# Attention with scores and weighted sums in turns, in three stretches of key tiles

## The chip, the cores and the metric

The kernel runs on one core of a Trainium2 chip. The core has a matrix engine (TensorE, PE in the profile, with its weight loads as PEld), a vector engine (VectorE, DVE), an engine for activations (ScalarE, ACT), a general one (GpSimd, POOL) and one that issues most DMAs (SyncE, SP). Each engine runs its own queue of instructions in order and waits on semaphores for the others. Matmuls write to PSUM, eight banks of 512 float32 values per partition; everything else lies in SBUF. The metric is the device time of one execution in microseconds, the median of several runs.

## What is computed

One transformer block on 2048 rows of 256 values: cross-attention with 16 heads of 64 over 1601 context rows plus one learned null key and value, with a residual, then a feed-forward part with weights of +1 and -1.

```python
x = layernorm(x);  a = layer_norm(x, g_norm)
q = a @ Wq;  k, v = split(context @ Wkv)            # 16 heads of 64
k = concat(null_k, k);  v = concat(null_v, v)       # 1602 keys
sim = (q * s) @ (k * s).T                           # s = 64 ** -0.25, masked
out = softmax(sim) @ v
x = x0 + layer_norm(out @ Wout, g_out)
h = relu(s0 * concat(y, -y) @ w(k0)) * 2            # y = layernorm(x), w = +-1
x = x + s2 * (relu(s1 * h @ w(k1)) * 2) @ w(k2)
```

## The kernel before

The attention part works in 32 units. A unit is a pair of heads p (eight of them) and a block b of 512 query rows (four of them). Keys come in 13 tiles of 128 (the last has 66), counted by k.

For a unit, `exps` (L284) computes the transposed scores of key tile k: two heads side by side in the rows of the array, 64 each, into a PSUM tile sT of two banks, and ACT takes the exponential into an SBUF tile e. The first two tiles also add a shift (L307) so that the exponential stays in range, and the stored keys are differences, so the shift stays in the accumulating banks for later tiles. `weighted` (L312) multiplies e with the values and adds over all 13 tiles in one PSUM tile av; two heads lie side by side in the columns of the array. GpSimd adds the 13 tiles e into acc (L498, L500), the denominators before the last sum over partitions.

The shift of a unit is the maximum of its scores, found one unit earlier: `max_chunk` (L251) computes the scores of 128 queries and some 400 keys in the faster float32r, and DVE reduces them; 16 chunks make a unit. `max_combined` (L264) joins them, `max_turned` (L269) turns them to rows and multiplies with `fan`, a stored 128 x 4 x 128 pattern of ones and zeros, into mT.

PSUM has two pools of two tiles each, two banks to a tile: `spare` (sT, av, po) and `flex` (max chunks, den, mt, psq). A tile is taken in turn, and its first writer waits until the last reader of the tile before it is done.

All of this stands in a schedule written by hand: the order in the program is the order on every engine. The loop over units (from L463) does, for each unit:

- 13 times `exps`, each with one max chunk of the next unit behind it, two behind tiles 0, 4 and 8 (`extra`)
- `max_combined` for the next unit, and in units 0 and 1 the normalisation of input rows two blocks ahead (`input_normed`), in unit 30 that of a finished block
- 13 times `weighted`; after tile 2, `divided` (L331) of the unit before: den on PE (L334), then on DVE the reciprocal (L336) and the product with avs (L337) into aoT
- in units 28 and 29 the weights w0 of the feed-forward part (L526, L528), in unit 0 some small scalars
- ACT copies av into avs (L542); then the projections of the next pair's values and keys (in blocks 0, 1 and 2), `project_out` of the unit before (po, L324, added into y_sb at L329), `max_turned`, and `project_q` for the unit after the next (psq at L196, then ACT writes qr at L197 and qT at L198)

qr is what the max chunks of the next unit but one read; qT is what its scores read. The feed-forward part follows after the last unit, with its own order (from L627).

Of the kernel before, what the change touches and what calls it, by code (L numbers as in the profile page):

```python
# [22 lines left out]
HEADS, DH = 16, 64  # L23
# [12 lines left out]
def xattn_ffn(ctx, tc, x, ctxT, mask, g_norm, null_kv, wq, wkv, wout, g_out, k0, k1, k2, s0, s1, s2, out):  # L36
# [12 lines left out]
    def spare(name):  # L49
        return ps_s.tile([128, 2, 512], F32, tag="s", name=name)  # L50
# [52 lines left out]
    def norm_root(b):  # L103
        mv, r = norms[b]
        nc.scalar.activation(r, mv[:, :, 1], AF.Sqrt, bias=eps_sb)
# [37 lines left out]
    with ExitStack() as att:  # L143
# [12 lines left out]
        maskb = ap.tile([128, KC], F32, name="maskb")  # L156
        ones_r = ap.tile([128, 128], F32R, name="ones_r")
        mcol = ap.tile([128, 128], F32, name="mcol")
        fan = ap.tile([128, 4, 128], F32, name="fan")
        pick = ap.tile([128, 4], F32, name="pick")  # L160

        weights = {}

# [105 lines left out]
        def max_turned(p, b):  # L269

            ps = flex(f"mt_{p}_{b}")
            nc.tensor.transpose(ps[:, 0, :128], mcol, ident)
            shifts[p, b] = wp.tile([128, 512], F32R, tag="mT", name=f"mT_{p}_{b}", bufs=1)
            nc.vector.tensor_tensor(
                shifts[p, b].rearrange("p (t q) -> p t q", t=4),
                ps[:, 0:1, :128].to_broadcast([128, 4, 128]),
                fan,
                ALU.mult,
            )

        def rows_of(k):
            return 128 if k < KC - 1 else KLAST
# [26 lines left out]
            nc.scalar.activation(e[:n], ps[:n], AF.Exp, bias=maskb[:n, k : k + 1])  # L309
            return e  # L310

        def weighted(p, k, e, av):  # L312
            v = pairs[p][1]
            n = rows_of(k)
            for j in range(2):
                nc.tensor.matmul(  # L316
                    av[ts(j, DH), 0, :], v[:n, k, ts(j, DH)], e[:n, j, :], start=k == 0, stop=k == KC - 1
                )

        def project_out(p, b, aoT):  # L320
            po = spare(f"po_{p}_{b}")
# [6 lines left out]
            else:  # L328
                nc.vector.tensor_tensor(y, pv, y, ALU.add)  # L329

        def divided(p, b, avs, acc, ps):  # L331

            for j in range(2):
                nc.tensor.matmul(ps[ts(j, DH), :], ones, acc[:, j, :], start=True, stop=True)  # L334
            aoT = lp.tile([128, 512], F32, tag="aoT", name=f"aoT_{p}_{b}", bufs=1)
            nc.vector.reciprocal(aoT, ps)  # L336
            nc.vector.tensor_tensor(aoT, avs, aoT, ALU.mult)  # L337
            return aoT

# [26 lines left out]
                nc.vector.tensor_scalar_mul(xnT[:, b, 1, :], pt[:, 1, :], gn_sb[:, 1:2])  # L366

        units = [(p, b) for p in range(NP) for b in range(NB)]
        extra = {0, 4, 8}

        ahead = {0: ((0, 1), (0,)), 1: ((2, 3), (1,)), 2: ((), (2, 3)), 3: ((), ())}

# [39 lines left out]
        nc.gpsimd.memset(mcol, 0.0)  # L412
        nc.gpsimd.memset(maskb, 0.0)
        nc.gpsimd.memset(ones, 1.0)
        nc.gpsimd.memset(fan, 1.0)

        nc.scalar.activation(warm, eps_sb, AF.Sqrt)

        open_pair(0)
        xn = input_root(0)  # L420
        nc.vector.tensor_scalar(ones_r, ident, 0.0, 1.0, ALU.mult, ALU.add)
        nc.vector.tensor_tensor(pick, ident[:, 0:4], ident[:, DH : DH + 4], ALU.add)
        input_normed(0, *xn)
        project_k(0, 0, slot)
        input_turned(0, slot)
# [17 lines left out]
        nc.vector.tensor_scalar(  # L443
            maskb[:KLAST, KC - 1 : KC], mcol_u8[:KLAST, KC - 1 : KC], -MASKED, MASKED, ALU.mult, ALU.add
        )
        for t in range(4):
            nc.vector.tensor_scalar_mul(fan[:, t, :], fan[:, t, :], pick[:, t : t + 1])
        for n in (2, 3):
            for t in range(4):
                max_chunk(0, 0, 4 * t + n, slot)  # L450
# [11 lines left out]
        with tc.manual_schedule():  # L462
            for u, (p, b) in enumerate(units):  # L463
                nxt = units[u + 1] if u + 1 < len(units) else None
                if b == 0 and p + 1 < NP:
                    load_pair(p + 1)
                    open_pair(p + 1)
                if u == len(units) - 5:
                    k0_u8 = xnT[:, 0].rearrange("p c q -> p (c q)").bitcast(U8)
                    k0_u8 = k0_u8.rearrange("p (c f) -> p c f", f=FF)  # L470
                    nc.sync.dma_start(out=k0_u8, in_=k0.rearrange("(c p) f -> p c f", p=128))
                if u == len(units) - 2:
                    k1_u8 = xnT[:, 2:4].rearrange("p b c q -> p (b c q)").bitcast(U8)
                    k1_u8 = k1_u8.rearrange("p (c f) -> p c f", f=FF)
                    k2_u8 = xnT[:, 1, 0, :].bitcast(U8).rearrange("p (c f) -> p c f", f=D)
                    nc.sync.dma_start(out=k1_u8, in_=k1.rearrange("(c p) f -> p c f", p=128))
                    nc.sync.dma_start(out=k2_u8, in_=k2.rearrange("(c p) f -> p c f", p=128))
                if nxt is None:

                    y0, x0 = y_sb[:, 0:4, :], x_sb[:, 0:4, :]  # L480
                    nc.gpsimd.tensor_tensor(y0, y0, gout_sb.unsqueeze(1).to_broadcast([128, 4, D]), ALU.mult)
                    nc.gpsimd.tensor_tensor(x0, x0, y0, ALU.add)

                es, n = [], 0
                acc = lp.tile([128, 2, 512], F32, tag="acc", name=f"acc_{p}_{b}")
                for k in range(KC):
                    if k == 0:

                        odd = spare(f"sT_{p}_{b}_1")
                        sT = [spare(f"sT_{p}_{b}_0"), odd]  # L490
                    es.append(exps(p, b, k, sT))
                    for _ in range(2 if k in extra else 1):
                        if nxt is not None:
                            max_chunk(*nxt, n)
                            n += 1
                    m = rows_of(k)
                    if k == 1:
                        nc.gpsimd.tensor_tensor(acc, es[0], es[1], ALU.add)  # L498
                    elif k > 1:
                        nc.gpsimd.tensor_tensor(acc[:m], acc[:m], es[k][:m], ALU.add)  # L500
                if nxt is not None:
                    max_combined(*nxt)
                else:
                    norm_begin(0, x_sb, "r")
                    norm_root(0)
                    norm_end(0, y_sb, x_sb, beside=True)
                if u == len(units) - 2:
                    norm_begin(0, y_sb, "y")
                    norm_root(0)
                    norm_end(0, y_sb, y_sb, beside=True)  # L510

                    nc.scalar.activation(warm, eps_sb, AF.Exp)
                if u < 2:
                    input_normed(u + 2, *input_root(u + 2), beside=True)
                    nc.scalar.activation(warm, eps_sb, AF.Exp)

                av = spare(f"av_{p}_{b}")
                for k in range(KC):
                    weighted(p, k, es[k], av)
                    if k == 2 and last is not None:  # L520
                        aoT = divided(*last, flex(f"den_{p}_{b}")[:, 0, :])
                if u in (len(units) - 4, len(units) - 3):

                    half = k0_u8[:, 2 * (len(units) - 3 - u) :, :][:, 0:2, :]
                    if u == len(units) - 4:
                        nc.vector.tensor_scalar_mul(w0, half, sgn[:, 0:1])  # L526
                    else:
                        nc.vector.scalar_tensor_tensor(  # L528
                            w0, half, sgn[:, 0:1], w0.bitcast(F32), ALU.mult, ALU.subtract
                        )  # L530
                        nc.vector.tensor_scalar_mul(s1b[:, 0:1], sgn[:, 1:2], 2.0)
                        nc.vector.tensor_scalar_mul(s1b[:, 1:2], sgn[:, 1:2], -1.0)
                if u == 0:


                    nc.vector.tensor_scalar(sgn, s_sb[:, 0:2], 0.0, None, ALU.is_ge)
                    nc.vector.tensor_scalar(sgn, sgn, 2.0, -1.0, ALU.mult, ALU.add)
                    nc.vector.tensor_tensor(s_sb[:, 0:2], s_sb[:, 0:2], sgn, ALU.mult)
                    nc.vector.tensor_scalar(s_out, s_sb[:, 0:1], s_sb[:, 1:2], 8.0, ALU.mult, ALU.mult)
                    nc.vector.tensor_tensor(s_out, s_out, s_sb[:, 2:3], ALU.mult)  # L540
                avs = lp.tile([128, 512], F32, tag="avs", name=f"avs_{p}_{b}", bufs=1)
                nc.scalar.copy(avs, av[:, 0, :])  # L542

                if u < 2:
                    input_turned(u + 2)
                if p + 1 < NP:
                    for n in ahead[b][0]:
                        project_v(p + 1, n, spare if n % 2 else flex)
                    for n in ahead[b][1]:
                        project_k(p + 1, n, spare if n % 2 else flex)  # L550
                    if b == 2:
                        keys_stepped(p + 1)
                if nxt is None:
                    uT = turned(0)
                if last is not None:
                    project_out(*last[:2], aoT)
                if nxt is not None:
                    max_turned(*nxt)
                if u + 2 < len(units):
                    project_q(*units[u + 2])  # L560
                last = (p, b, avs, acc)
# [134 lines left out]
```

## Time and profile before

| | us |
|---|---|
| median of 3 runs (1352.63 to 1354.06) | 1352.65 |
| the profiled execution | 1355.55 |
| its span | 1353.7 |

The profiled execution stands 0.2% above the median; the 1.9 us between its time and its span lie outside the instructions. Attention takes the span up to about 1163 us, the feed-forward part the rest. The costliest groups, with the columns line, engine and operation, tiles and shapes, count, then busy time in us and mean in ns, then idle time before them and what ended it:

```profile
L500 POOL TENSOR_TENSOR acc<-acc,e 128x1024 f32<-128x1024 f32 (+1 forms) x352 | 847.3, 2407 | 27.6
L262 DVE TENSOR_REDUCE mx<-max 128x2 f32<-128x800 f32 (+1 forms) x512 | 481.3, 988 | 70.9 <-PE max L259 61.2
L309 ACT ACTIVATE e<-sT,maskb 128x1024 f32<-128x1024 f32 (+1 forms) x416 | 460.0, 1115 | 64.0 <-PE sT L296 38.0
L296 PE MATMUL sT<-qT,kT 64*128 64x512 f32 (+1 forms) x1664 | 444.4, 612 | 1.6 <-ACT e L309 1.4
L316 PE MATMUL av<-e,v 128*64 128x512 f32 (+1 forms) x1664 | 369.5, 594 | 1.0
L259 PE MATMUL max<-kr,qr 64*128 64x400 f32 (+1 forms) x1024 | 285.7, 568 | 2.3 <-DVE mx L262 1.5
```

Matmuls overlap, so a mean of 612 ns is the length of one record, not what one costs in the stream; the chain of waits shows the cost. Idle time in a group is that of its engine just before the instructions.

### The profile page before, as it was taken

How to read it: one execution, taken by the hardware profiler on the slowest of the kernel's cores; microseconds unless marked ns; L12 is line 12 of the kernel's file. 1: busy time of each engine (PE TensorE's matmuls, PEld its weight loads, DVE VectorE, ACT ScalarE, POOL GpSimd, SP SyncE). 2: the span in 40 equal slices, each digit the busy share in tenths (PEclk: the TensorE clock that was granted, in tenths of full speed). 3: DMA queues.
4: the chain of work that ended last, by engine and by line, in shares of the span. 5: the costliest groups of instructions: out<-in, count | busy, mean ns of one | idle time of the engine just before them, and what ended most of it. 6: DMA issues, size and time to landing. Idle time of an engine off the chain costs nothing.

```text
span 1353.7 us, 16255 instructions
## 1 busy us (share of the span) xinstructions
PE 1329.3 (98%) x6528; PEld 664.6 (49%) x6528; DVE 880.7 (65%) x957; ACT 607.7 (45%) x655; POOL 994.8 (73%) x492
## 2 busy tenths in 40 slices
PE   6999999999999999999999999999999999999998
PEld 3544444444444444444444444444444443688887
DVE  5677776676667756686767656767676884464431
ACT  1666454445444454444544454454445557421220
POOL 4377987798888987798779877987798999711100
PEclk9799999999999999999999999999999999999999
DMA  5000000000000000000000000000000010000000
GB/s 136 4 1 7 0 1 8 8 1 0 8 1 7 1 1 8 7 1 1 7 8 1 1 8 8 0 1 5 0 16 1 1 39 0 1 0 16 16 16 16
DMA packets 14940, 12.31 MB, mean 9 GB/s; under 512 B 2240, under 2 KB 14784, under 8 KB 14864
## 3 DMA queue, kind: packets, MB, share of 16 engines
q1 hardware_dynamic: 13552, 9.70, 2.5%
q10 hardware_dynamic: 832, 1.23, 0.3%
q8 instruction: 51, 0.84, 0.3%
q0 software_dynamic: 480, 0.34, 0.1%
q14 instruction: 25, 0.20, 0.1%
HBM read 9.17 MB, written 2.10 MB: 8 GB/s over the span
## 4 chain that ended last, share of the span: by engine, by line
PE 93%; DVE 3%; ACT 2%; DMA 1%; issue 0%; POOL 0%; SPq 0%; ACTq 0%
PE sT L296 28%; PE av L316 27%; PE ps L592 10%; PE max L259 8%; PE psq L196 4%; PE po L324 4%; PE psv L230 3%; PE psk L207 3%; PE ps L615 2%; PE den L334 2%; ACT e L309 1%; PE sT L307 1%; DVE mx L262 1%; DMA x_sb<-in_x 1%; PE xT L361 0%
## 5 line engine op out<-in xcount | busy, mean ns | idle before, releaser
L500 POOL TENSOR_TENSOR acc<-acc,e 128x1024 f32<-128x1024 f32 (+1 forms) x352 | 847.3, 2407 | 27.6
L262 DVE TENSOR_REDUCE mx<-max 128x2 f32<-128x800 f32 (+1 forms) x512 | 481.3, 988 | 70.9 <-PE max L259 61.2
L309 ACT ACTIVATE e<-sT,maskb 128x1024 f32<-128x1024 f32 (+1 forms) x416 | 460.0, 1115 | 64.0 <-PE sT L296 38.0
L296 PE MATMUL sT<-qT,kT 64*128 64x512 f32 (+1 forms) x1664 | 444.4, 612 | 1.6 <-ACT e L309 1.4
L316 PE MATMUL av<-e,v 128*64 128x512 f32 (+1 forms) x1664 | 369.5, 594 | 1.0
L259 PE MATMUL max<-kr,qr 64*128 64x400 f32 (+1 forms) x1024 | 285.7, 568 | 2.3 <-DVE mx L262 1.5
L316 PEld LDWEIGHTS av<-e,v 128*64 128x64 f32 (+1 forms) x1664 | 116.7, 137 | 239.0 <-issue 219.3
L259 PEld LDWEIGHTS max<-kr,qr 64*128 64x128 f32 x1024 | 97.3, 186 | 187.2 <-DVE mx L262 149.7
L296 PEld LDWEIGHTS sT<-qT,kT 64*128 64x128 f32 (+1 forms) x1664 | 135.3, 181 | 104.8 <-ACT e L309 81.5
L498 POOL TENSOR_TENSOR acc<-e,e 128x1024 f32<-128x1024 f32 x32 | 75.5, 2358 | 147.6 <-ACT e L309 147.6
L542 ACT COPY avs<-av 128x512 f32<-128x512 f32 x32 | 18.8, 587 | 327.0 <-PE av L316 327.0
L336 DVE RECIPROCAL aoT<-den 128x512 f32<-128x512 f32 x31 | 104.1, 3357 | 70.0 <-PE den L334 70.0
L197 ACT ACTIVATE qr<-psq 128x512 fp32r<-128x512 f32 x32 | 19.1, 597 | 139.1 <-PE psq L196 139.1
L592 PE MATMUL ps<-h0hi,w 128*128 128x512 f32 x256 | 79.5, 392 | 0.0
L592 PE MATMUL ps<-h0lo,w 128*128 128x512 f32 x256 | 78.9, 389 | 0.0
L211 DVE TENSOR_TENSOR kT<-psk,keep 128x400 f32<-128x400 f32 (+1 forms) x32 | 18.4, 574 | 90.0 <-PE psk L207 89.8
L119 POOL TENSOR_TENSOR y_sb<-y_sb,gout_sb 128x256 f32<-128x256 f32 x12 | 9.3, 776 | 90.1 <-DVE y_sb L86 90.1
L581 DVE SCALAR_TENSOR_TENSOR h1lo<-ps,h1hi 128x1024 fp32r<-128x1024 f32 x16 | 19.6, 1224 | 69.0 <-ACT h1hi L580 69.0
L196 PE MATMUL psq<-xnT,wq 128*128 128x512 f32 x128 | 62.2, 610 | 0.6 <-DVE kT L211 0.6
L324 PE MATMUL po<-wo,aoT 128*128 128x256 f32 x256 | 61.5, 383 | 0.0
L329 DVE TENSOR_TENSOR y_sb<-po,y_sb 128x1024 f32<-128x1024 f32 x28 | 34.2, 1220 | 40.0 <-PE po L324 39.8
L580 ACT ACTIVATE h1hi<-ps 128x1024 fp32r<-128x1024 f32 x16 | 16.4, 1027 | 94.6 <-PE ps L592 94.6
(125 smaller groups left out, 1054.8 us busy)
## 6 DMA issues: line engine op xcount, KB each, us to landing
x_sb<-in_x SPq DMA_DIRECT2D x4, 512.0 KB, 8.7
out_x<-o SPq DMA_DIRECT2D x8, 256.0 KB, 2.1
wkv<-in_wkv SPq DMA_DIRECT2D x16, 96.0 KB, 2.1
wq<-in_wq SPq DMA_DIRECT2D x8, 128.0 KB, 2.3
wo<-in_wout SPq DMA_DIRECT2D x8, 128.0 KB, 2.1
xnT<-in_k SPq DMA_DIRECT2D x1, 1024.0 KB, 5.9
ctx_sb<-in_ctxT ACTq DMA_DIRECT2D x3, 300.0 KB, 7.9
xnT<-in_k SPq DMA_DIRECT2D x1, 512.0 KB, 3.9
```

Source lines behind the costliest of these rows:

```text
L196: nc.tensor.matmul(ps[:, 0, :], weights[p][0][:, c, :], xnT[:, b, c, :], start=c == 0, stop=c == 1)
L207: nc.tensor.matmul(ps[:, 0, :w], weights[p][1][:, c, 0, :], ctx_sb[:, c, keys], start=c == 0, stop=c == 1)
L259: nc.tensor.matmul(ps[:, j, :w], queries[p, b][1][rows, ts(t, 128)], pairs[p][2][rows, ds(start, w)], start=True, stop=True)
L262: nc.vector.tensor_reduce(maxima[p, b][:, t, :, c], ps[:, :, :w], AX.X, ALU.max)
L296: nc.tensor.matmul(ps[:n, j, :], kT[rows, ds(128 * k, n)], qT[rows, :], start=k < 2, stop=k >= 2, skip_group_check=k >= 2,)
L309: nc.scalar.activation(e[:n], ps[:n], AF.Exp, bias=maskb[:n, k : k + 1])
L316: nc.tensor.matmul(av[ts(j, DH), 0, :], v[:n, k, ts(j, DH)], e[:n, j, :], start=k == 0, stop=k == KC - 1)
L324: nc.tensor.matmul(pv[:, t, :], aoT[:, ts(t, 128)], weights[p][2], start=True, stop=True)
L336: nc.vector.reciprocal(aoT, ps)
L498: nc.gpsimd.tensor_tensor(acc, es[0], es[1], ALU.add)
L500: nc.gpsimd.tensor_tensor(acc[:m], acc[:m], es[k][:m], ALU.add)
L592: nc.tensor.matmul(ps[:, f, :], w(c)[:, ts(2 * g + f, 128)], parts[part][:, c, :], start=i == 0, stop=i == len(steps) - 1,)
```

## The change

The 13 key tiles are cut into three stretches. In each, some tiles of scores come first and then some of weighted sums: 4 and 3, 4 and 5, 5 and 5. The sums of a stretch have a PSUM tile of their own (flex, flex, spare): ACT copies the first into avs, DVE adds the other two to it. The max chunks are dealt out anew: one before tile 0 and one before tile 4 (`AHEAD`), the others behind tiles (`BEHIND`), none behind tiles 3 and 7. `divided` is parted: den and the reciprocal (`inverse`) come after the first weighted tile of the second stretch (k = 3), the product behind the scores of the third. The norms of units 0 and 1 stand behind the scores of the third stretch, that of unit 30 behind those of the second; `input_turned` comes after the projections. `fan` goes; mT is multiplied with `pick`, read again for each of the 128 columns. avs has two buffers.

```diff
-        fan = ap.tile([128, 4, 128], F32, name="fan")
-        pick = ap.tile([128, 4], F32, name="pick")
+        pick = ap.tile([128, 4, 1], F32, name="pick")
...
-                fan,
+                pick.to_broadcast([128, 4, 128]),
...
-        def weighted(p, k, e, av):
+        def weighted(p, k, e, av, start, stop):
...
+                nc.tensor.matmul(av[ts(j, DH), 0, :], v[:n, k, ts(j, DH)], e[:n, j, :], start=start, stop=stop)
...
-        def divided(p, b, avs, acc, ps):
+        def inverse(p, b, avs, acc, ps):
 
             for j in range(2):
                 nc.tensor.matmul(ps[ts(j, DH), :], ones, acc[:, j, :], start=True, stop=True)
             aoT = lp.tile([128, 512], F32, tag="aoT", name=f"aoT_{p}_{b}", bufs=1)
             nc.vector.reciprocal(aoT, ps)
+            return aoT
+
+        def divided(p, b, avs, acc, ps):
+
+            aoT = inverse(p, b, avs, acc, ps)
             nc.vector.tensor_tensor(aoT, avs, aoT, ALU.mult)
             return aoT
...
-        extra = {0, 4, 8}
+
+        STRETCHES = ((range(0, 4), range(0, 3)), (range(4, 8), range(3, 8)), (range(8, 13), range(8, 13)))
+
+        AHEAD = {0: 1, 4: 1}
+        BEHIND = {0: 1, 1: 2, 2: 1, 4: 1, 5: 2, 6: 1, 8: 1, 9: 1, 10: 1, 11: 1, 12: 2}
...
-        nc.gpsimd.memset(fan, 1.0)
...
-        for t in range(4):
-            nc.vector.tensor_scalar_mul(fan[:, t, :], fan[:, t, :], pick[:, t : t + 1])
...
-                for k in range(KC):
-                    if k == 0:
-
-                        odd = spare(f"sT_{p}_{b}_1")
-                        sT = [spare(f"sT_{p}_{b}_0"), odd]
-                    es.append(exps(p, b, k, sT))
-                    for _ in range(2 if k in extra else 1):
+                avs = lp.tile([128, 512], F32, tag="avs", name=f"avs_{p}_{b}")
+
+                odd = spare(f"sT_{p}_{b}_1")
+                sT = [spare(f"sT_{p}_{b}_0"), odd]
+
+                def chunks(count):
+                    nonlocal n
+                    for _ in range(count if nxt is not None else 0):
+                        max_chunk(*nxt, n)
+                        n += 1
+
+                for i, (scores, sums) in enumerate(STRETCHES):
+                    for k in scores:
+                        chunks(AHEAD.get(k, 0))
+                        es.append(exps(p, b, k, sT))
+                        chunks(BEHIND.get(k, 0))
+                        m = rows_of(k)
+                        if k == 1:
+                            nc.gpsimd.tensor_tensor(acc, es[0], es[1], ALU.add)
+                        elif k > 1:
+                            nc.gpsimd.tensor_tensor(acc[:m], acc[:m], es[k][:m], ALU.add)
+                    if i == 2:
                         if nxt is not None:
-                            max_chunk(*nxt, n)
-                            n += 1
...
+                            max_combined(*nxt)
+                        else:
+                            norm_begin(0, x_sb, "r")
+                            norm_root(0)
+                            norm_end(0, y_sb, x_sb, beside=True)
+                        if last is not None:
+                            nc.vector.tensor_tensor(aoT, last[2], aoT, ALU.mult)
+                        if u < 2:
+                            input_normed(u + 2, *input_root(u + 2), beside=True)
+                            nc.scalar.activation(warm, eps_sb, AF.Exp)
+                    if u == len(units) - 2 and i == 1:
+                        norm_begin(0, y_sb, "y")
+                        norm_root(0)
+                        norm_end(0, y_sb, y_sb, beside=True)
+
+                        nc.scalar.activation(warm, eps_sb, AF.Exp)
+                    av = (flex, flex, spare)[i](f"av_{p}_{b}_{i}")
+                    for k in sums:
+                        weighted(p, k, es[k], av, k == sums[0], k == sums[-1])
+                        if k == 3 and last is not None:
+                            aoT = inverse(*last, flex(f"den_{p}_{b}")[:, 0, :])
+                    if i == 0:
+                        nc.scalar.copy(avs, av[:, 0, :])
+                    else:
+                        nc.vector.tensor_tensor(avs, av[:, 0, :], avs, ALU.add)
...
-                avs = lp.tile([128, 512], F32, tag="avs", name=f"avs_{p}_{b}", bufs=1)
-                nc.scalar.copy(avs, av[:, 0, :])
-
-                if u < 2:
-                    input_turned(u + 2)
+
                 if p + 1 < NP:
...
+                if u < 2:
+                    input_turned(u + 2)
```

More of the change, by code (lines that the diff above doesn't have):

```diff
@@ L315, in weighted @@
             for j in range(2):
-                nc.tensor.matmul(
-                    av[ts(j, DH), 0, :], v[:n, k, ts(j, DH)], e[:n, j, :], start=k == 0, stop=k == KC - 1
-                )
+                nc.tensor.matmul(av[ts(j, DH), 0, :], v[:n, k, ts(j, DH)], e[:n, j, :], start=start, stop=stop)
         def project_out(p, b, aoT):
@@ L421, in xattn_ffn @@
         nc.vector.tensor_scalar(ones_r, ident, 0.0, 1.0, ALU.mult, ALU.add)
-        nc.vector.tensor_tensor(pick, ident[:, 0:4], ident[:, DH : DH + 4], ALU.add)
+        nc.vector.tensor_tensor(pick[:, :, 0], ident[:, 0:4], ident[:, DH : DH + 4], ALU.add)
         input_normed(0, *xn)
@@ L485, in xattn_ffn @@
                 acc = lp.tile([128, 2, 512], F32, tag="acc", name=f"acc_{p}_{b}")
-                for k in range(KC):
-                    if k == 0:
-                        odd = spare(f"sT_{p}_{b}_1")
-                        sT = [spare(f"sT_{p}_{b}_0"), odd]
-                    es.append(exps(p, b, k, sT))
-                    for _ in range(2 if k in extra else 1):
-                        if nxt is not None:
-                            max_chunk(*nxt, n)
-                            n += 1
[L496 to L512, printed above, removed]
-                if u < 2:
-                    input_normed(u + 2, *input_root(u + 2), beside=True)
-                    nc.scalar.activation(warm, eps_sb, AF.Exp)
@@ L517, in xattn_ffn @@
[L517 to L521, printed above, removed]
+                avs = lp.tile([128, 512], F32, tag="avs", name=f"avs_{p}_{b}")
[6 more added lines that the diff above has]
+                        n += 1
@@ L540, in xattn_ffn @@
                     nc.vector.tensor_tensor(s_out, s_out, s_sb[:, 2:3], ALU.mult)
-                avs = lp.tile([128, 512], F32, tag="avs", name=f"avs_{p}_{b}", bufs=1)
-                nc.scalar.copy(avs, av[:, 0, :])
-                if u < 2:
-                    input_turned(u + 2)
                 if p + 1 < NP:
```

## The prediction

> **What bounds the kernel now.** I read the page's shares and groups first, then the waits, then the chain of waits over one (pair, block) unit, because 98% of busy PE can hide stretched matmuls.
>
> ```profile
> PE 1329.3 (98%) x6528; PEld 664.6 (49%) x6528; DVE 880.7 (65%) x957; ACT 607.7 (45%) x655; POOL 994.8 (73%) x492
> ...
> PE 93%; DVE 3%; ACT 2%; DMA 1%; issue 0%; POOL 0%; SPq 0%; ACTq 0%
> ```
>
> ```profile
> PEld max L259 <- DVE mx L262: 149.7, 343, 1.4
> ...
> PEld sT L296 <- ACT e L309: 81.5, 197, 1.1
> ```
>
> So PE carries the chain, but in the score loop it is held by DVE (a max buffer comes free) and by ACT (a score buffer comes free). The chain of one unit gives the prices (start, length, what):
>
> ```profile
> 609.94 1.29 PE av L316 x6
> 611.23 1.92 PE po L324 x8
> 613.15 0.11 PE mt L272
> 613.26 1.72 PE psq L196 x4
> 614.98 1.06 PE sT L296 x4
> 616.04 0.23 PE sT L307
> ...
> 618.86 0.18 PE max L259
> 619.04 1.12 PE sT L296 x4
> 620.16 0.18 PE max L259 x2
> 620.34 0.93 PE sT L296 x4
> 621.27 0.61 PE max L259 x4
> 621.88 0.86 PE sT L296 x4
> ...
> 630.24 1.12 ACT e L309
> 631.37 0.04 issue
> 631.41 2.79 PE av L316 x11
> ```
>
> Prices on PE: a key tile of scores 0.86 us, of weighted sums 4 x 0.215 = 0.86, the shift 0.23, a max chunk 0.18. What exceeds them is waiting: 1.12 and 0.93 for scores are ACT, 0.61 for two chunks instead of 0.36 is DVE. A third excess has no waiter: the first score tile after psq takes 1.06 where 0.86 is its price, and po takes 1.92 for eight matmuls of 0.215 (1.72). Each time the tiling of the array changes (128 rows x 128 columns to 64 rows, 64 columns to 128), 0.20 us go.
>
> From one psq end to the next a unit without projections of the next pair takes 32.4 us (the one from 1037.69 to 1070.11): scores 16.38, sums with the denominator 12.28, tail 3.75. The bare stream is 13 x 0.857 + 16 x 0.183 + 2 x 0.23 = 14.53 for the scores, 14 x 0.857 = 12.0 for the sums, 3.75 tail: 30.28. So 2.1 us a unit are open to gain at most, 0.2 of them the switch after psq, 0.26 the switch and wait before the sums, 1.66 the waits of the score loop.
>
> ACT and DVE around a unit's start:
>
> ```profile
> 615.08 0.60 ACT L197 ACTIVATE qr<-psq 128x512 fp32r<-128x512 f32 x1 [3.22 <-PE psq L196]
> 615.57 0.59 ACT L198 ACTIVATE qT<-psq 128x512 f32<-128x512 f32 x1
> ```
>
> **What the skill says.** The Trainium skill, "TensorE: Matmul & The Clock Gate", section "The mechanism" of its Part 3, says that a weight load overlaps running matmuls only when the row groups differ, and that matmuls never change order. The trace agrees with both: the load for the first score tile starts with the tile (614.91), and the 0.20 are exposed. "SBUF — State Buffer", section "Who interferes with whom", has a DVE tensor_tensor with both inputs in SBUF contend with GpSimd's reads, the second one waiting. The product L337 is such a one: 0.69 us at least, 1.75 median, 2.90 at most, the long ones where POOL's 2.36 us additions run. The new additions read one input from PSUM, as L329 does, which takes 1.21 to 1.23 us for 1024 columns; I take 0.7 us for 512 and no lock. "PSUM — Partial Sum Buffer", section "Engine vs sequencer instructions", says that ACT's, DVE's and POOL's queues are strict FIFO; so what stands ahead of a reduction delays it.
>
> **The change, step by step.** Time runs from psq's end. Latencies, from the unit at 614.98: qr ends at 0.70; a chunk ends 0.50 after what releases its buffer (or qr); a reduction starts 0.05 after its chunk, and they follow at 0.90; an exponential takes 1.11 and starts 0.11 after its scores; scores that wait for a buffer end 1.17 after the exponential that frees it. These rules give c2 of the unit above its end at 3.02, as the trace has it.
>
> *First stretch (scores 0 to 3, chunks c0 to c4).* Before, scores 0 came first and covered qr. Now c0 stands ahead of them: it needs qr, which only the psq just done feeds. PE is in order, so c0 ends at 0.70 + 0.50 = 1.20 instead of 0.38 (switch and chunk): 0.82 lost. Then scores 0 at 2.06, shift 2.29, c1 2.49, scores and shift 1 at 3.58, c2 3.78, c3 waits for c0's and c1's reductions: 4.02; scores 2 at 4.88, c4 waits for c2's reduction (4.81): 5.31, scores 3 at 6.17. Sums 0 to 2: switch 0.20 + 2.57 = 8.94. ACT's copy of av (9.0 to 9.6) frees its buffer before c6 wants it.
>
> *Second stretch.* Switch and c5 9.32, scores 4 at 10.18, c6 10.36, scores 5 11.22, c7 11.40, c8 waits for c6's reduction 11.90, scores 6 12.76, c9 12.94, scores 7 13.80. Sums 3 to 7 with den: 0.20 + 6 x 0.857 = 19.15. The reciprocal starts at 15.8, ends at 19.1 just as the sums do; the addition into avs ends at 19.9.
>
> *Third stretch.* Scores 8 at 20.21, c10 needs that addition: 20.40, met exactly. Then ACT limits: scores 10 at 22.61, 11 at 23.72, 12 at 25.0, and c14, c15 end at 25.43. Sums: 29.91. DVE: last reduction 27.11, mcol 27.33, product 28.1 to 30.3, hidden but for up to 0.5 us where it meets POOL.
>
> Tail 3.75 as before: 33.66 against 32.41, +1.25 us a unit. In other words scores 17.31 (were 16.38): the short stretches recover about 0.3 of the waits, and c0 costs 0.82 and two switches 0.40. Sums 12.60 (were 12.28): three entries at 0.20 instead of one of 0.26. The switches into sums and back have no direct row; bounds are 0 (loads wholly ahead) and 0.25 (max to av before, part of it ACT). I take 0.20, which psq to sT and av to po show. With 31 units that have a next one: +38.8.
>
> *The odd units.* In units 0 and 1 the norm of later rows (DVE 2.3, then eight ACT operations of 0.5 and a 1.28 table load, 105.0 to 114.0) hid under 12 us of sums; now under 4.3. ACT is done at about 35 to 37 after the start, so v's copies, the turned rows and psq wait: 5 and 4 us. Nothing moves it earlier; bounds 2 and 12 together. In units 28 and 29 w0 (3.38 and 4.45 us on DVE) follows a product that now ends at 28 to 30 instead of early in the sums; y_sb and mT come late, and c0 needs mT's buffer: 3.5 together, bounds 0 and 6. In unit 30 the norm of y (9 us of ACT, 1120.0 to 1129.0) now has 5.4 us of sums before exponential 8 queues behind it: 3. The last unit has no chunks: two stretches' sums let ACT catch up (about 1 us), four more switches take 0.8: nothing.
>
> Edits with one answer: fan's four multiplications (0.28 each) and its memset go from the start, where ACT's table load ends later anyway: -0.4, between -0.9 and 0. mT multiplies by a broadcast instead of a stored tile, same size: nothing. POOL's twelve additions a unit (29 us) still fit into 33.7; SP's queue is untouched. Product against POOL: 31 units, one in ten or so late: 1 (0 to 15).
>
> Sum: 38.8 + 9 + 3.5 + 3 + 1 - 0.4 = 54.9. The profiled execution took 1355.55 (span 1353.7): 1410.4. The median of the runs is 2.9 lower: 1408.
>
> **The rivals.**
> *A, forecast*, 1408, range 1394 to 1421: 0.55.
> *B, slower by less*: the switches cost nothing (4 x 0.2 x 31 = 25 less), or the first chunk's wait is covered (0.82 x 31 = 25 less): 1383. For it: max to av shows 0.26 with ACT in it; against: the exposure is 0.20 on psq to sT in every unit. 0.21.
> *C, slower by more*: the late product meets POOL's addition in every unit, +0.5 x 31 = 15: 1423. For it: half of the products took 2.9; against: 2.2 us of slack. 0.10.
> *D, faster*: DVE and ACT work off their arrears while PE does sums, so the score loop's 1.66 of waits vanish, c0 included. Then a unit is 30.28 + 6 x 0.2 = 31.5, 28 less over 31 units: 1325 (1340 if the odd units still pay). It decides as soon as the score waits of a unit fall below about 0.9 from my 2.15. For it: the 149.7 and 81.5 us of waits. Against: the arrears begin again inside each stretch, as two buffers are all there are. 0.11.
> *E, a draw*, gains and switches cancel: 1352: 0.03. That the order is not as written is no rival: the schedule is manual, each engine's order is the program's.
>
> **How the numbers follow.** The likeliest is 1408. The range 1376 to 1423 holds A, B and most of C; D and E (0.14) and C's end stay out. A measurement of this kernel can tell 0.2% (2.7 us) from no change: faster 0.11, same 0.03, slower 0.86.
>
> **What would show it.** The waits: a new line, max weights for qr, 0.8 us x 31; av weights, and scores behind av, 0.2 late. By unit 33.6 us where it was 32.4. DVE's wait for max and PE's for e stay of the order they have. I am wrong if the first chunk ends within 0.5 us of psq, or if scores after sums take 0.86 with no switch, or if the stretches of four take under 4.2 us.

## The result, and the profile after

| | before | after |
|---|---|---|
| median of 4 runs, us | 1352.86 (1352.63 to 1354.06) | 1406.05 (1404.61 to 1406.75) |
| profiled execution, us | 1355.55 | 1404.61 |
| its span, us | 1353.7 | 1402.8 |

The changed kernel takes 1.039 times as long (95% interval 1.0372 to 1.0408), 53.2 us more by the medians and 49.1 by the spans of the two profiles (the profiled execution of the kernel before lies 2.7 us above its median, that of the changed kernel 1.4 below). The page of the changed kernel, first its busy times, then the shares of the chain:

```profile
PE 1336.6 (95%) x6528; PEld 668.1 (48%) x6528; DVE 952.7 (68%) x1017; ACT 600.5 (43%) x655; POOL 993.3 (71%) x491
...
PE 80%; DVE 10%; ACT 8%; issue 1%; DMA 1%; POOL 0%; ACTq 0%; SPq 0%; DVEq 0%
```

PE had 93% of the chain and has 80; DVE and ACT now hold 18% of the way to the end. By their busy times they do little more than before (DVE 72 us, ACT 7 less): PE waits for them at places where it had other work. The waits of the changed kernel (who waited for whom, us in total, times, longest) say for which:

```profile
PEld max L258 <- DVE mx L261: 88.5, 187, 2.0
...
PEld sT L295 <- ACT e L308: 56.7, 100, 2.2
...
PEld max L258 <- ACT qr L196: 47.5, 30, 2.0
...
PE max L258 <- ACT qr L196: 16.3, 22, 0.7
```

The two waits that the turns could relieve, 149.7 and 81.5 before, did fall. The wait of a max chunk for qr is 47.5; before, it was:

```profile
PEld max L259 <- ACT qr L197: 6.9, 24, 1.5
```

The chain of waits from the end of one psq on (start, length, what) shows where a unit pays:

```profile
638.13 0.02 issue
...
638.21 0.61 ACT qr L196
638.82 0.04 issue
638.86 0.45 PE max L258 x2
639.31 0.86 PE sT L295 x4
...
643.39 0.86 PE sT L295 x4
644.25 2.73 PE av L315 x12
646.97 0.38 PE max L258 x2
...
653.70 3.43 PE av L315 x16
657.14 1.08 PE sT L295 x4
```

From psq's end at 638.13 to the end of the first chunk at 639.31 pass 1.18 us, of which the chunk itself needs 0.18 and the change of tiling 0.20. Twelve weighted matmuls take 2.73 where 12 x 0.214 = 2.57 is their price; the chunk after them takes 0.38, not 0.18; scores after sums take 1.08, not 0.86. Each change of tiling between scores and sums costs.

From the ends of the matmul records the whole difference can be laid out (us; a unit runs from psq's end to the next one's):

| stretch of the run | before | after | difference |
|---|---|---|---|
| up to the first unit | 51.45 | 47.66 | -3.8 |
| unit 0 | 36.14 | 40.87 | +4.7 |
| unit 1 | 36.74 | 43.69 | +7.0 |
| units 2 to 27 | 913.37 | 941.89 | +28.5 |
| units 28 and 29 | 64.83 | 67.75 | +2.9 |
| unit 30 | 30.71 | 34.41 | +3.7 |
| unit 31, to its last sum | 28.86 | 28.48 | -0.4 |
| from there to the last matmul | 187.37 | 193.73 | +6.4 |

The first row is not the change's. It differs by nearly as much between the runs below (48.3 to 51.4, among kernels made from either side), and in the records it is a pace: psq and a psv of the same shape took 2.83 and 3.78 us there in the one profile and 1.88 and 2.37 in the other. The pace is that of the clock granted to TensorE, the third number from the end in these sums over a stretch (from 40 us to the first unit), before and after:

```profile
40.00:51.45 11.45, 11.35 (x44) 7.86 (x43) 5.86 (x8) 2.95 (x6) 0.00 (x0) 0.56 0.01 1
40.00:47.66 7.66, 7.50 (x37) 5.46 (x37) 4.38 (x7) 2.37 (x5) 0.00 (x0) 0.76 0.00 0
```

In the runs below it is 0.56 to 0.59 in that stretch where the first unit begins after 50 us, and 0.71 to 0.74 where it begins before 49.

In a unit between 2 and 27 the scores take 6.14 + 4.86 + 6.22 = 17.22 us (16.38 before), the sums 2.73 + 5.30 + 4.44 = 12.47 (12.28 before), and the tail what it took, but for units of the last block (and 28 and 29), which have no projections and where it takes 3.95 instead of 3.75. The end of such a unit in the chain:

```profile
629.52 1.90 DVE mx L261 x2
...
631.45 0.19 DVE mcol L266
631.63 2.56 DVE aoT L519
634.19 0.14 issue
634.32 1.97 PE po L321 x8
```

The product (L519), last on DVE, begins during a POOL addition and ends half a microsecond behind it (2.62 us median, 1.75 before), and po begins 0.2 us late for it. In the other units the projections stand ahead of po and cover this.

Unit 1 shows what the norms do when only 4.4 us of sums lie behind them. Its chain near the end:

```profile
115.64 2.46 DVE aoT L519
...
120.78 1.98 DVE nm L137
122.76 0.60 DVE avs L537
...
123.41 3.03 PE psk L206 x4
```

The product, the statistics and the norm's little operation nm (128 x 4 values, 2.06 us; it ends with the POOL addition that ran when it began) stand ahead of the last addition into avs on DVE; psk needs the PSUM tile that this addition frees, and PE waits. psk itself in that unit, before and after, in the timeline (in brackets the idle time ahead of it and its releaser):

```profile
119.26 1.51 PE L207 MATMUL psk<-ctx_sb,wkv 96*128 96x400 f32 x4
123.41 3.03 PE L206 MATMUL psk<-ctx_sb,wkv 96*128 96x400 f32 x4 [2.83 <-DVE avs L537]
```

The sums over the stretch behind that wait:

```profile
123.00:129.00 6.00, 5.59 (x15) 3.97 (x16) 1.56 (x3) 5.84 (x13) 0.00 (x0) 0.50 0.00 0
```

So the wait is only about half of what unit 1 loses beyond the other units. After PE had stood for 2.8 us the granted clock was 0.50 from 123 to 129 us (1.00 up to 122), and psk, the turned rows and po took 7.0 us in place of 4.1.

After unit 31 the feed-forward part begins with the turned rows uT, which need the last norm; in the timeline:

```profile
1206.23 0.41 PE L127 MATMUL uT<-ident,y_sb 128*128 128x128 f32 x2 [1.49 <-issue]
1207.13 0.44 PE L127 MATMUL uT<-ident,y_sb 128*128 128x128 f32 x2 [0.49 <-ACT y_sb L141]
1209.06 0.69 PE L127 MATMUL uT<-ident,y_sb 128*128 128x128 f32 x2 [1.49 <-ACT y_sb L141]
1210.99 0.69 PE L127 MATMUL uT<-ident,y_sb 128*128 128x128 f32 x2 [1.24 <-ACT y_sb L141]
```

Before, the eight ran without a gap (1162.02, 1.09 us), as ACT had finished the norm under 12 us of sums. Here too the clock follows: it was 0.50 from 1208 to 1214 us, and the eight matmuls of po behind the turned rows took 3.2 us in place of 1.7.

### The profile page after: what moved, and what is told of

Its sections match the earlier page's. It is cut to its first block, busy times and chain, and to the rows that moved or that the text cites. A ratio compares the mean times of both kernels' runs of the same rounds, so it can differ in the third digit from the quotient of the medians.

```text
span 1402.8 us, 16362 instructions
## 1 busy us (share of the span) xinstructions
PE 1336.6 (95%) x6528; PEld 668.1 (48%) x6528; DVE 952.7 (68%) x1017; ACT 600.5 (43%) x655; POOL 993.3 (71%) x491
## 4 chain that ended last, share of the span: by engine, by line
PE 80%; DVE 10%; ACT 8%; issue 1%; DMA 1%; POOL 0%; ACTq 0%; SPq 0%; DVEq 0%
PE av L315 24%; PE sT L295 21%; PE ps L606 9%; PE max L258 7%; ACT e L308 5%; DVE mx L261 4%; PE po L321 3%; PE psq L195 3%; PE psk L206 3%; PE psv L229 3%; PE ps L629 2%; PE den L331 2%; PE sT L306 1%; DVE aoT L519 1%; DVE kr L211 1%
## 5 line engine op out<-in xcount | busy, mean ns | idle before, releaser
L261 DVE TENSOR_REDUCE mx<-max 128x2 f32<-128x800 f32 (+1 forms) x512 | 492.9, 990 | 180.3 <-PE max L258 174.5
L308 ACT ACTIVATE e<-sT,maskb 128x1024 f32<-128x1024 f32 (+1 forms) x416 | 453.7, 1114 | 276.3 <-PE sT L295 223.5
L295 PE MATMUL sT<-qT,kT 64*128 64x512 f32 (+1 forms) x1664 | 434.5, 599 | 6.0 <-ACT e L308 2.9
L315 PE MATMUL av<-e,v 128*64 128x512 f32 (+1 forms) x1664 | 383.6, 598 | 0.0
L258 PE MATMUL max<-kr,qr 64*128 64x400 f32 (+1 forms) x1024 | 276.2, 555 | 29.5 <-ACT qr L196 16.3
L315 PEld LDWEIGHTS av<-e,v 128*64 128x64 f32 (+1 forms) x1664 | 111.0, 136 | 238.0 <-issue 180.2
L295 PEld LDWEIGHTS sT<-qT,kT 64*128 64x128 f32 (+1 forms) x1664 | 143.0, 182 | 99.3 <-ACT e L308 56.7
L519 DVE TENSOR_TENSOR aoT<-avs,aoT 128x512 f32<-128x512 f32 x31 | 78.7, 2539 | 0.0
L595 DVE SCALAR_TENSOR_TENSOR h1lo<-ps,h1hi 128x1024 fp32r<-128x1024 f32 x16 | 19.6, 1223 | 69.0 <-ACT h1hi L594 69.0
L206 PE MATMUL psk<-ctx_sb,wkv 96*128 96x400 f32 (+1 forms) x128 | 52.1, 540 | 8.8 <-DMA ctx_sb<-in_ctxT 4.8
L321 PEld LDWEIGHTS po<-wo,aoT 128*128 128x128 f32 x256 | 49.2, 196 | 21.2 <-PE av L315 9.1
L594 ACT ACTIVATE h1hi<-ps 128x1024 fp32r<-128x1024 f32 x16 | 16.4, 1025 | 94.5 <-PE ps L606 94.5
```

Source lines behind the costliest of these rows:

```text
L206: nc.tensor.matmul(ps[:, 0, :w], weights[p][1][:, c, 0, :], ctx_sb[:, c, keys], start=c == 0, stop=c == 1)
L258: nc.tensor.matmul(ps[:, j, :w], queries[p, b][1][rows, ts(t, 128)], pairs[p][2][rows, ds(start, w)], start=True, stop=True)
L261: nc.vector.tensor_reduce(maxima[p, b][:, t, :, c], ps[:, :, :w], AX.X, ALU.max)
L295: nc.tensor.matmul(ps[:n, j, :], kT[rows, ds(128 * k, n)], qT[rows, :], start=k < 2, stop=k >= 2, skip_group_check=k >= 2,)
L315: nc.tensor.matmul(av[ts(j, DH), 0, :], v[:n, k, ts(j, DH)], e[:n, j, :], start=start, stop=stop)
L321: nc.tensor.matmul(pv[:, t, :], aoT[:, ts(t, 128)], weights[p][2], start=True, stop=True)
```

## The experiments

Each ran in three rounds beside the kernel before on the same chip.

### The first chunk, in both kernels

```diff
-        AHEAD = {0: 1, 4: 1}
-        BEHIND = {0: 1, 1: 2, 2: 1, 4: 1, 5: 2, 6: 1, 8: 1, 9: 1, 10: 1, 11: 1, 12: 2}
+        AHEAD = {4: 1}
+        BEHIND = {0: 2, 1: 1, 2: 1, 3: 1, 4: 1, 5: 2, 6: 1, 8: 1, 9: 1, 10: 1, 11: 1, 12: 2}
```

> The changed kernel with its first chunk behind key tile 0 instead of ahead of it (two behind tile 0, one behind tiles 1, 2 and 3). Theory (the first chunk waits for qr with nothing to cover it, 0.8 us in each of 31 units, and the array switches and odd units make the rest): the first stretch of scores falls from 6.14 to about 5.35 us, the other stretches stay, the time falls by 24 us to 1382. Rival 1 (turns are a gain, only this chunk stands wrongly): 1355 or less. Rival 2 (the additions of partial sums and the late product carry the loss): 1400 or more.

Measured: 1381.41 us, ratio 1.0214 (1.0199 to 1.023). The first stretch takes 5.36 us, the second and third 4.86 and 6.22 as they were. The wait of the chunk's weights for qr falls back:

```profile
PEld max L258 <- ACT qr L196: 6.5, 22, 1.5
```

The counterpart puts that piece alone into the kernel before:

```diff
-        extra = {0, 4, 8}
+        extra = {4, 8}
...
+                    if k == 0 and nxt is not None:
+                        max_chunk(*nxt, n)
+                        n += 1
                     es.append(exps(p, b, k, sT))
```

> The kernel before with one edit: of the two max chunks behind key tile 0, one goes ahead of it. Theory: PE waits for qr in each of 31 units with nothing to do, the score stretch goes from 16.38 to about 17.2 us: 24 us more, 1377. Rival (DVE and ACT set the pace of the score loop, and DVE gets its first chunk earlier, so the wait is hidden): 1350 to 1358.

Measured: 1379.27, ratio 1.0188 (1.0173 to 1.0203), 26 us more; the score stretch takes 17.18 us (16.38 before). PE now waits for qr at a unit's start as the changed kernel does:

```profile
625.55 1.73 PE psq L196 x4
...
627.37 0.60 ACT qr L197
...
628.02 0.45 PE max L259
628.47 0.86 PE sT L296 x4
```

So a chunk ahead of the first scores costs 0.8 us a unit with or without turns: 25 of the 53 us. DVE and ACT, busy as they are in this loop, do not hide it.

### The change of tiling alone

In the kernel before, one max chunk goes amid the sums.

```diff
-                        if nxt is not None:
+                        if nxt is not None and n < 15:
                             max_chunk(*nxt, n)
                             n += 1
-                if nxt is not None:
-                    max_combined(*nxt)
-                else:
+                if nxt is None:
                     norm_begin(0, x_sb, "r")
...
                     weighted(p, k, es[k], av)
+                    if k == 6 and nxt is not None:
+                        max_chunk(*nxt, n)
+                        max_combined(*nxt)
```

> The kernel before with one edit: the last of the 16 max chunks goes from behind the last key tile of scores to behind weighted tile 6, amid the sums, and the maxima are joined after it. It adds one change of the array's tiling there and one back. Theory: each pair of changes takes 0.34 us beside the chunk's 0.18; the score stretch ends where it did, as ACT sets its end, so the sums grow from 12.28 to 12.8 us and the time by 11 to 16 us: 1363 to 1369. Rival (weights are loaded ahead and the change of tiling is free): 6 us more at most, 1353 to 1358.

Measured: 1370.84, ratio 1.0139 (1.0112 to 1.0166), 18 us more, a little above what was expected. The chain of this kernel, around the chunk:

```profile
641.76 3.43 PE av L316 x16
645.20 0.38 PE max L259 x2
645.57 5.30 PE av L316 x24
```

The chunk takes 0.38 where 0.18 is its price, and the 24 matmuls behind it 5.30 where they take 24 x 0.2142 = 5.14 in a row: 0.20 to leave the sums, 0.15 to come back. The scores end only 0.18 earlier, for the chunk that is gone, and the sums start 0.17 later behind ACT, as no chunk fills that wait any more. Together 0.53 us a unit; in six of the seven units of the last block that have a next one it is 0.9, as their scores take some 0.6 longer, for which the runs show no reason. That makes 18.5 us over the 31 units, and the medians differ by 18. What is shown for the change of tiling itself is the 0.35 a pair.

### Partial sums without turns

All scores first; sums, additions, reciprocal and product as in the changed kernel.

```diff
-        STRETCHES = ((range(0, 4), range(0, 3)), (range(4, 8), range(3, 8)), (range(8, 13), range(8, 13)))
-        AHEAD = {0: 1, 4: 1}
-        BEHIND = {0: 1, 1: 2, 2: 1, 4: 1, 5: 2, 6: 1, 8: 1, 9: 1, 10: 1, 11: 1, 12: 2}
+        STRETCHES = ((range(13), range(0, 3)), ((), range(3, 8)), ((), range(8, 13)))
+        AHEAD = {}
+        BEHIND = {k: 2 if k in (0, 4, 8) else 1 for k in range(KC)}
...
-                    if i == 2:
+                    if i == 0:
                         if nxt is not None:
                             max_combined(*nxt)
...
-                        if last is not None:
-                            nc.vector.tensor_tensor(aoT, last[2], aoT, ALU.mult)
-                        if u < 2:
+                    if i == 2 and last is not None:
+                        nc.vector.tensor_tensor(aoT, last[2], aoT, ALU.mult)
+                    if i == 0 and u < 2:
...
-                    if u == len(units) - 2 and i == 1:
+                    if u == len(units) - 2 and i == 0:
```

> The changed kernel with all 13 tiles of scores in the first stretch (chunks dealt out as in the kernel before, norms behind the scores) and the sums still in three parts of 3, 5 and 5, each with its own PSUM tile, added up in SBUF, reciprocal one part ahead of the product. Theory: partial sums, additions and the parted reciprocal cost nothing where PE does not change between scores and sums: score stretch 16.4 us, sums 12.2 to 12.3, tail 3.75 to 3.95, time 1351 to 1356. Rival (additions and late product carry the loss): most of the 53 us stay, 1380 or more.

Measured: 1390.15, ratio 1.0278 (1.0253 to 1.0304), as the rival had it and not the theory. But the profile does not say that additions cost: units 2 to 27 take 917.8 us together, 4.4 more than before. The loss sits in units 1, 30 and 31, whose sums took 22.2, 21.6 and 19.6 us, and the waits name it:

```profile
PE den L331 <- ACT avs L535: 20.0, 3, 7.1
```

With the norm ahead of the sums, ACT's copy of the first partial sum queues behind 5 to 9 us of norm, and den needs the PSUM tile that the copy frees. The edit had made a new wait of its own. The next two runs carried the same fault: one took units 0, 1, 30 and 31 out of the turns, the other also moved the first chunk.

```diff
+                plain = u < 2 or u >= len(units) - 2
+                stretches = PLAIN if plain else STRETCHES
+                ahead_of, behind_of = ({}, PLAIN_BEHIND) if plain else (AHEAD, BEHIND)
-                for i, (scores, sums) in enumerate(STRETCHES):
+                for i, (scores, sums) in enumerate(stretches):
```

> The changed kernel with units 0, 1, 30 and 31 as in the run without turns, the other 28 in turns. Theory: the norms of these units and the weights behind them find 12 us of sums again; the tails of units 0 and 1 fall by 4 and 6 us, the third stretch of unit 30 by 2, the time up to the feed-forward part by 6, and four units' share of the steady loss goes: 22 us less, 1384. Rival (the loss is the same in every unit and nothing else): 4 us less, 1402.

Measured: 1416.86, ratio 1.0483 (1.0465 to 1.05).

> Both edits together: first chunk behind tile 0, and units 0, 1, 30 and 31 without turns. Theory: the two add up, 22 + 22 us less: 1362, still some 9 us over the kernel before, from four more switches of the array in each of 28 units (0.34 us a pair) less what the short stretches gain. Rival 1 (turns are a gain once both hindrances are gone): below 1350. Rival 2 (neither carries the loss): above 1390.

Measured: 1393.11, ratio 1.0301 (1.0285 to 1.0316). In both, den waits for that copy in three units, 20.0 us in all, and the sums of units 1, 30 and 31 take 20 to 22 us. They decide nothing between the theories. Mended, with maxima and norms behind the first three weighted tiles and their copy (`i == 1` in place of `i == 0`):

> As the run without turns, but the maxima, the norms and their table loads stand behind the first three weighted tiles and their copy into avs, so ACT's copy is not queued behind 5 to 9 us of norm, and den does not wait for that copy's PSUM tile. Theory (in units 1, 30 and 31 that queue alone made the sums 19.6 to 22.2 us long; the other units show 12.42 us, 0.13 more than before): these sums fall to about 12.5, time 1355 to 1361. Rival (partial sums themselves disturb these units): stays above 1375.

Measured: 1362.02 against 1355.1 in the same rounds, ratio 1.0059 (1.0038 to 1.008). The long sums are gone (12.3 to 12.4 us). A unit's sums in the chain of this run:

```profile
103.17 3.60 PE av L315 x16
106.77 1.00 PE den L331 x4
107.77 7.73 PE av L315 x36
```

They take 12.33 instead of 12.2 in that unit, 0.14 of it at den. Units 2 to 27 come to 917.9, 4.5 over before; unit 30's scores take 18.2 us (16.4 before), as w0 on DVE makes mT late. So partial sums, additions and the parted reciprocal cost 0.17 us a unit when nothing else moves; they are not what makes the changed kernel slow.

### The odd units, mended

> Units 0, 1, 30 and 31 without turns, with the norms behind the first copy into avs, the other units in turns as in the changed kernel. Theory: the odd units' own loss goes (3 us in unit 0, 6 in unit 1, 3 in unit 30, 6 behind unit 31): 1387 to 1390. Rival (these units lose no more than others): 1402.

Measured: 1389.09, ratio 1.0259 (1.0239 to 1.0278). Unit 0 falls from 40.9 to 37.4 us, unit 1 from 43.7 to 36.9, unit 30 from 34.4 to 32.7, and the part behind the last sum from 193.7 to 186.7. Together that is 19 us, in which the three units' share of the loss of every unit is contained; by the medians the run is 17 us shorter than the changed kernel.

> The same with the first chunk behind tile 0 in the units with turns. Theory: the two edits add up, 18 us under the 1381 of the first chunk's move alone: 1362 to 1365, so some 10 us over the kernel before, 0.25 to 0.45 us in each of 27 units from the added changes of tiling. Rival 1 (turns are a gain once the hindrances are gone): below 1350. Rival 2 (they do not add up): above 1372.

Measured: 1367.88, ratio 1.01 (1.0074 to 1.0125), some 3 us above the range expected (which, over 1352.7, was 1.007 to 1.009). By its profile the first stretch is 5.36 and the odd units are as in the run above. The excess lies in three places. Unit 0 gives back 1.5 us and not 3, as moving the chunk alone had already shortened it (from 40.9 to 38.9). Unit 30's scores take 18.0 us, because w0 on DVE still makes mT late. And in seven units of the first block (4, 8 and on to 28) the third stretch takes 6.50 in place of 6.22, 1.9 us in all: its first exponential starts late, behind a max chunk.

```profile
ACT e L308 <- PE max L258: 38.6, 7, 5.5
...
639.57 0.19 issue
639.75 1.12 ACT e L308
```

This is no effect of the moved chunk: the run above has the same 6.50 and the same line. The wait, seven times, is in every run in which the changed kernel has units without turns (with no turns at all it costs the same seven units 0.27 us of their scores), and in no other; why it arises stays open.

Turns in 28 units, with both hindrances gone, are still slower than none: units 2 to 27 take 922.3 us, 917.9 without turns and 913.4 before. The changed kernel's loss of 1.10 us in each of these units so parts into 0.82 for the first chunk (941.9 against 920.5 with the chunk behind tile 0), 0.17 for the turns, and 0.11 for partial sums and what goes with them (the 0.17 without turns, less the late exponential, which the changed kernel does not have). The four added changes of tiling take an estimated 0.7 (twice 0.15 and twice 0.20, from the lengths above), so the turns do relieve the waits, by about 0.5 us a unit, and that is less than they cost. No version here is faster than the kernel before.

## Why the prediction was right

It said 1408 us; measured are 1406.05, and the mechanism it led with is the one that the runs show. The steps, in its order:

- *The first chunk waits for qr, 0.82 us a unit.* Right. It ends 1.18 to 1.20 after psq, as worked out, in most units (1.35 in those of the last block, where it also waits for mT on DVE), and the two runs that move it, one in each kernel, give 25 and 26 us.
- *The stretches.* 6.17, 4.86 and 6.28 us of scores forecast, 6.14, 4.86 and 6.22 measured. The rules of latency that it took from one unit before hold.
- *Relief by turns.* Right in size for the unit: without the first chunk and two switches, the scores would be 17.22 - 0.82 - 0.39 = 16.0, against 16.38. That the waits for DVE and ACT would keep their order was wrong, though: they fell from 231 to 145 us. Those waits are the weight loads'; the score loops before lost only 1.85 us a unit against their bare stream, 57 us in 31 units, so most of the 231 us lay under matmuls that still ran, and 86 us less of them gave some 0.4 us a unit.
- *Changes of tiling, 0.20 each.* Out of sums into scores 0.20 (0.62 instead of 0.43 to the end of the first matmul, in every one of 33 cases); into sums only 0.15 (0.572 to 0.575 to the end of the first matmul, in all of 96 cases). Three of the latter a unit: that and the smaller wait of the third stretch make the steady loss 1.10 us instead of 1.25, over 26 units 4 us less.
- *What the Trainium skill says on loads* ("TensorE: Matmul & The Clock Gate", section "The mechanism"). That a load overlaps only where row groups differ does not fit this trace, and the step was wrong to say that the trace agrees: in the sums every load uses all rows and takes 0.14 us, and 16 matmuls still take 16 x 0.214 us, so their loads lie under running matmuls. What is not hidden here comes with a change of tiling; the measurement decides.
- *Units 0 and 1.* Forecast 5 and 4 us beyond the steady loss; 3.6 and 5.9 measured. Unit 1's order of causes was another: PE waits at psk for the last addition into avs on DVE, which the step did not name, and half of the loss is the slower clock behind that wait, which no step had.
- *Units 28, 29 and 30.* Forecast 3.5 for w0 and 3 for unit 30's norm; w0 delayed mT by 0.5 us after each unit, some 1 us and not 3.5, and unit 30 lost 2.1 in its third stretch to the norm.
- *Product against POOL, 1 us, one in ten.* An addition held the product in 30 of 31 units; that made po late only in the nine units without projections of the next pair, by 0.2 each, some 2 us. So rival C's ground was there, and its cost was not.
- *The last unit, nothing.* The unit itself, -0.4, fits; but its norm was forgotten. It feeds the feed-forward part's first transposes, and 6.4 us were lost there, the wait and the slower clock behind it together.
- *The start, -0.4.* -3.8, but not by the change: the granted clock was 0.56 before the first unit in one profile and 0.76 in the other. fan's multiplications themselves gave nothing, as DVE then waited 4.0 us for ACT instead of 3.2.

That the sum is closer than its parts is luck. The forgotten norm, 6.4 us, stands against a start 3.4 us lower than forecast, 0.15 us less in each of 31 units and some 2.5 less for w0: 54.9 forecast, 49.1 between the two profiled executions, 53.2 between the medians.

Rival B had two grounds, and the runs speak against both: a change of tiling is not free (0.38 for a chunk amid the sums), and the first chunk's wait is not covered (25 and 26 us). Rival D, the one of a gain, needed the score waits of a unit to fall below 0.9 us. They did not, even with the first chunk moved: 5.36 + 4.86 + 6.22 is 1.9 above the bare 14.53, 0.6 of it three changes of tiling, which leaves 1.3 of waits.

## What to carry to other kernels

In the score loop here three engines stood near their limit (of 16.4 us, PE has 14.5, ACT 13 exponentials of 1.11 and DVE 16 reductions of 0.99), and being cut and interleaved gave it less than it cost: each piece fills and drains the same two buffers, and every turn pays the array's change of tiling, 0.15 us one way and 0.20 the other. Ahead of such a cut, ask of each moved instruction what hid its wait; here one chunk moved by one place cost 25 us of the 53, several times what the turns cost in net. And work that lay under a long stretch of another engine, such as a norm or a table load, has to be placed anew when that stretch is cut, together with the small copies that would queue behind it; here, where PE then stood for some 3 us, the matmuls behind ran at half the clock for some 6 us more.

## What was not expected of the hardware

- The change of the array's tiling is not symmetric: 64-row tiles with 128 columns to 128 rows with 64 columns takes 0.146 us, back 0.195, each time it was seen without another wait.
- A product of two SBUF tiles on DVE and an addition on POOL did not share the time: one ran through and the other waited, and where their starts lay more than 0.01 us apart, the one that began first ran through. In the kernel before, 28 products began within 0.1 us of an addition. In 14 of them the product took 0.69 us and the addition some 2.9; in the other 14 the addition took some 2.4 and the product 2.87 to 2.90. In the changed kernel, where 29 of 31 products began some 0.3 us after an addition had, they took 2.55 to 2.64 and ended 0.55 behind it. An operation on 128 x 4 values (nm) took 0.14 alone and 2.06 that way, while the additions into avs, with one input from PSUM, took 0.62 to 0.69 in all 64 cases.
- After 2.8 us in which PE had no matmul, the granted clock was 0.50 for about 6 us, with PE busy again for 5.6 of them.
